# Second feed-forward product straight to nodes on the partitions, residual from rows, first norms on VectorE, all planning constants new

## The chip, the cores and the metric

The kernel runs on one core of a Trainium2 chip. The metric is the time of one execution on the device in microseconds (us); where several were made, the median is quoted.

In the lines of profiles, PE is TensorE (PEld its weight loads), DVE is VectorE, ACT is ScalarE, POOL is GpSimd, and SPq is the queue of SyncE, which issues transfers. `out<-in` names the tiles written and read, and L1089 is a line of the kernel.

## The reference, cut to what matters

Sixteen graphs share one adjacency matrix. Three graph-attention layers are followed by one transformer layer with eight heads, two feed-forward products and two layer norms. The change is in the last lines and in the very first norm.

```python
# x: (16, 1024, 256) float32, adj: (1024, 1024)
h = jnp.maximum(_layernorm(x, axis=-1), 0.0)             # the first norm
x = x + _L0_gnn_ref(h, adj, ...)                         # 4 heads
# ... layers 1 and 2 alike, with one head each ...
# layer 3 (cut): q, k, v = split(x @ w_qkv); 8 heads, masked softmax over the 1024 nodes; t = attention output
x = _layernorm(x + t, ln1_g, ln1_b)
h = jax.nn.relu(jnp.einsum('fnc,cd->fnd', x, w1) + b1)
f_out = jnp.einsum('fnd,dc->fnc', h, w2) + b2
x = _layernorm(x + f_out, ln2_g, ln2_b)
```

## The kernel before

The kernel records every operation with a guessed duration, and then plans the order itself. It runs a list scheduler over all five engines, in which each stretch of a batch has a rising priority given by fitted constants (`GATS`, `VALUES`, `STEPS`, `FEED`, `LEAD`, `BIAS`). The engines then work through that order.

In the last layer, queries and keys are split into a high and a low part, and both are moved by SyncE into stacks of operands for the score products. A projection (one of queries or keys, for one of two head groups `g` and one node half `hf`) makes 16 moves of 64 KB. There is one buffer `hi` and one buffer `lo`:

```python
        def project(g, hf, keys, stack, at):
            sc, hi, lo = r_sc.new(), r_hi.new(), r_lo.new()
            # ... two products into sc (PSUM) on TensorE ...
            act(act_us(HALF), lambda: nc.scalar.copy(hi.t.bitcast(F32R), sc.t), [hi], [sc])
            dve(tt_us(HALF), lambda: nc.vector.tensor_sub(lo.t, sc.t, hi.t), [lo], [sc, hi])
            for a in range(4):
                part = ((hi, hi, lo, lo), (hi, lo, hi, lo))[keys][a]
                for r in range(HG):
                    dma(0.33, lambda: nc.sync.dma_start(
                            stack.t[a * D3 : (a + 1) * D3, r, at : at + HALF],
                            part.t[r * D3 : (r + 1) * D3, :]),
                        [stack((r, hf if keys else 0, a))], [part], us=0.635)
```

The softmax denominators are sums of exponentials over nodes. In the second node half of each head group, two of each four tiles are added by transfers of 512 KB that accumulate while they write, issued by GpSimd. There are 16 of them in each batch except the last, 240 in all:

```python
        def run_of(g, hf):
            return 1 if b == NB - 1 else 4 if hf == 1 else 2
        # ... for each of the 8 tiles jt of a stage (g, hf):
                if jt % run == 1:
                    # ... VectorE starts the sum of a run: sums = pas[m - 1] + pas[m] ...
                elif jt % run:
                    for ss, pt in zip(sums[g, hf], pas[m]):
                        dma(3.0, lambda: nc.gpsimd.dma_start(ss.t, pt.t, accum_op=ALU.add),
                            [ss], [pt], us=0.88, engine="pool")
```

The feed-forward part kept channels on the partitions up to the residual, and then transposed back:

```python
        def forward(hf):
            yT = yTs[hf]                          # normed rows, transposed, with gain and bias
            fT = [r_fz.new() for _ in range(CT)]
            # ... first product and Relu into fT ...
            for co in range(CT):
                g = r_bank.new()
                pe(CT * mm_us(HALF), lambda: product(g, co, w2_sb, lambda ct: fT[ct].t), [g], fT)
                u = yT.t[:, co, :]
                dve(stt_us(HALF), lambda: nc.vector.scalar_tensor_tensor(
                        u, g.t, cols["b2"][:, co : co + 1], u, op0=ALU.add, op1=ALU.add), [yT(co)], [g])
        def back(hf):
            # ... four transposes of yT per pair of node tiles into a PSUM bank ...
            # ... ScalarE copies each tile to SBUF with accum_out (the sum for the norm), then the norm ...
```

## Time and profile before

| | before |
|---|---|
| median of 3 runs | 4160.25 us (4156.57 to 4164.75) |
| profiled execution | 4150.3 us |
| mean granted TensorE clock | 0.991 |
| streaming of all TensorE records, by their start-to-start times | 3,822 us |
| mean time of a steady batch (14 of them) | 251.2 us |

A steady batch is the time from the first one-head graph-attention product of one batch to that of the next, read from the trace. One more number is the **loss**. I add up what the TensorE records should take back to back (0.43 us for width 512, and so on), and about 0.35 us for each visit to the column-tiled form (records marked `128*32`, of which four take the time of one full product). The time by which TensorE's starts fall behind that sum is loss: 46 us in ten steady batches, 4.6 us a batch.

### The profile page before, as it was taken

How to read it: one execution, taken by the hardware profiler on the slowest of the kernel's cores; microseconds unless marked ns; L12 is line 12 of the kernel's file. 1: busy time of each engine (PE TensorE's matmuls, PEld its weight loads, DVE VectorE, ACT ScalarE, POOL GpSimd, SP SyncE). 2: the span in 40 equal slices, each digit the busy share in tenths (PEclk: the TensorE clock that was granted, in tenths of full speed). 3: DMA queues.
4: the chain of work that ended last, by engine and by line, in shares of the span. 5: the costliest groups of instructions: out<-in, count | busy, mean ns of one | idle time of the engine just before them, and what ended most of it. 6: DMA issues, size and time to landing. Idle time of an engine off the chain costs nothing.

```text
span 4150.3 us, 68028 instructions
## 1 busy us (share of the span) xinstructions
PE 4049.7 (98%) x23874; PEld 2358.5 (57%) x23874; DVE 3504.5 (84%) x5994; ACT 2680.9 (65%) x6673; POOL 558.7 (13%) x631
## 2 busy tenths in 40 slices
PE   7899999999999999999999999999999999999998
PEld 3746556564665646556464665646556465564643
DVE  7498888988889898898988889888897988889866
ACT  4556667576766756667566665756667566575665
POOL 0001111111111101111111111111111111111110
PEclk9999999999999999999999999999999999999999
DMA  3124444344443424443254443434434244442441
GB/s 105 37 67 103 116 96 102 77 90 105 100 109 84 103 78 100 114 105 95 69 112 108 97 102 88 92 92 100 110 92 100 71 103 119 98 95 65 98 111 47
DMA packets 215246, 389.63 MB, mean 94 GB/s; under 512 B 45168, under 2 KB 80240, under 8 KB 214896
## 3 DMA queue, kind: packets, MB, share of 16 engines
q1 hardware_dynamic: 180336, 259.36, 22.3%
q0 software_dynamic: 34560, 125.84, 16.0%
q8 instruction: 190, 3.11, 0.3%
q14 instruction: 160, 1.31, 0.1%
HBM read 91.03 MB, written 33.95 MB: 30 GB/s over the span
## 4 chain that ended last, share of the span: by engine, by line
PE 79%; ACT 8%; DVE 6%; DMA 2%; SPq 2%; issue 2%; POOL 0%; DVEq 0%; ACTq 0%
PE bank L840 18%; PE bank L1161 12%; PE sc L1295 10%; PE bank L927 10%; PE bank L716 7%; PE bank L512 5%; PE bank L937 5%; PE bank L1392 5%; PE sc L1077 4%; ACT waste L429 2%; PE sc L1113 2%; SPq L1098 2%; DVE pa L1328 2%; ACT pa L1319 1%; DVE pt L813 1%
## 5 line engine op out<-in xcount | busy, mean ns | idle before, releaser
L1319 ACT ACTIVATE pa<-sc 128x512 f32<-128x512 f32 x2048 | 1108.1, 607 | 448.7 <-PE sc L1295 317.5
L1328 DVE TENSOR_TENSOR pa<-pa,mask 128x1024 f32<-128x1024 f32 x1024 | 1221.9, 1220 | 72.9 <-ACT pa L1319 68.6
L813 DVE SCALAR_TENSOR_TENSOR pt<-row,e,mask 128x512 f32<-128x512 f32 x1536 | 1068.1, 747 | 49.6 <-DMA row<-rd 35.8
L840 PE MATMUL bank<-qb,pt 128*128 128x257 f32 x4096 | 943.9, 383 | 1.4 <-DVE pt L813 1.0
L840 PEld LDWEIGHTS bank<-qb,pt 128*128 128x128 f32 x4096 | 780.5, 191 | 143.8 <-ACT pa L1319 11.7
L1295 PE MATMUL sc<-qs,ks 128*128 128x512 f32 x2048 | 702.8, 451 | 39.1 <-DVE lo L1089 35.7
L1295 PEld LDWEIGHTS sc<-qs,ks 128*128 128x128 f32 x2048 | 361.2, 190 | 288.1 <-issue 91.2
L1161 PE MATMUL bank<-pa,va 128*32 128x512 f32 x4096 | 514.7, 597 | 1.3 <-DVE pa L1328 1.0
L927 PE MATMUL bank<-pt,qb 128*32 128x512 f32 x4096 | 502.2, 596 | 4.3 <-DVE pt L813 3.4
L1188 DVE TENSOR_TENSOR sums<-pa,pa 128x1024 f32<-128x1024 f32 x360 | 435.6, 1221 | 30.3 <-PE bank L1161 25.3
L716 PE MATMUL bank<-w_aug,hT 128*128 128x259 f32 (+1 forms) x1536 | 391.2, 393 | 2.1 <-ACT hT L710 1.9
L1196 POOL DMA_DIRECT2D sums<-pa x240 | 210.5, 877 | 1059.4 <-DVE rec L860 239.0
L716 PEld LDWEIGHTS bank<-w_aug,hT 128*128 128x128 f32 x1536 | 283.9, 192 | 110.3 <-ACT pa L1319 12.6
L868 ACT ACTIVATE ex<-bank,rec 128x256 f32<-128x256 f32 x256 | 123.4, 482 | 303.3 <-DVE rec L860 302.6
L927 PEld LDWEIGHTS bank<-pt,qb 128*32 128x32 f32 x4096 | 122.3, 109 | 296.5 <-issue 224.0
L937 PE MATMUL bank<-pt,e 128*32 128x512 f32 x2048 | 278.6, 594 | 0.0
L1161 PEld LDWEIGHTS bank<-pa,va 128*32 128x32 f32 x4096 | 116.4, 109 | 256.7 <-issue 216.9
L1077 PE MATMUL sc<-hTa,wqkv_sb 128*128 128x512 f32 x512 | 244.5, 602 | 1.6 <-ACT pa L1319 0.8
L483 ACT ACTIVATE hn<-xt,mv,rstd 128x256 f32<-128x256 f32 x384 | 203.3, 597 | 51.6 <-DVE mv L456 30.0
L429 ACT ACTIVATE waste<-xt,mv 128x256 f32<-128x256 f32 x384 | 196.2, 511 | 7.0
L1161 PE MATMUL bank<-sums,ones 128*32 128x512 f32 x1440 | 193.5, 599 | 0.2 <-DMA sums<-pa 0.2
L1086 ACT CAST hi<-sc 128x512 fp32r<-128x512 f32 x128 | 74.5, 582 | 178.9 <-PE sc L1077 76.9
(119 smaller groups left out, 4305.9 us busy)
## 6 DMA issues: line engine op xcount, KB each, us to landing
sums<-pa POOLq DMA_DIRECT2D x240, 512.0 KB, 5.9
row<-rd SPq DMA_DIRECT2D x192, 256.0 KB
ks<-hi SPq DMA_DIRECT2D x512, 64.0 KB
ks<-lo SPq DMA_DIRECT2D x512, 64.0 KB
qs<-hi SPq DMA_DIRECT2D x512, 64.0 KB
qs<-lo SPq DMA_DIRECT2D x512, 64.0 KB
xt<-in_x_dram SPq DMA_DIRECT2D x32, 512.0 KB
x<-xt SPq DMA_DIRECT2D x32, 512.0 KB
```

The lines of the kernel that those rows point to most:

```text
L429: lambda: nc.scalar.activation(waste.t, src, AF.Square, bias=sums[:, k : k + 1], accum_out=squares[:, k : k + 1]),
L716: nc.tensor.matmul(g.t[:, : C + 3 * H], hT.t[:, ct, k * P : (k + 1) * P], w_aug[l][:, ct, :], start=ct == 0, stop=ct == CT - 1,)
L813: lambda: nc.vector.scalar_tensor_tensor(pt.t, row.t, e3[:, 2, jt // TH, h, jt % TH : jt % TH + 1], mask[:, jt, hf * HALF : (hf + 1) * HAL ...
L840: nc.tensor.matmul(g.t[:, : D + 1], pts[jt].t[:, k * P : (k + 1) * P], qb[:, jt, 0, :], start=jt == 0, stop=jt == NT - 1,)
L927: nc.tensor.matmul(g.t[u * D + d : u * D + d + D3, :], qb[:, j, h + u, d : d + D3], pts[u][j - jt].t, start=j == 0, stop=j == NT - 1,)
L937: nc.tensor.matmul(gd.t[c : c + D3, :], one(jt + k, h + u).to_broadcast([P, D3]), pts[u][k].t, start=jt == 0, stop=jt == NT - 2,)
L1077: nc.tensor.matmul(sc.t, wqkv_sb[:, ct, c0 : c0 + P], hT.t[:, ct, hf * HALF : (hf + 1) * HALF], start=ct == 0, stop=ct == CT - 1,)
L1161: nc.tensor.matmul(ac.t[r * D3 : (r + 1) * D3, :], columns(r), of_head(r), start=first, stop=last,)
L1188: lambda: nc.vector.tensor_add(ss.t, p0.t, p1.t),
L1295: nc.tensor.matmul(scs[r - r0].t, ks.t[:, r, jt * P : (jt + 1) * P].bitcast(F32R), q.t[:, r, :].bitcast(F32R), start=True, stop=True,)
L1319: lambda: nc.scalar.activation(pt.t[:, v, :], sc.t, AF.Exp, scale=1.0 / math.sqrt(D3)),
L1328: lambda: nc.vector.tensor_mul(pt.t, pt.t, mask[:, jt : jt + 1, i0 : i0 + HALF].to_broadcast([P, 2, HALF]),),
```

## The change

TensorE bounds the kernel, so work is taken from it. The second product takes the Relu output as its stationary operand, so that nodes come out on the partitions at once and the transposes back go. The residual is then needed as rows, with gain and bias multiplied in by VectorE, and `b2` is folded into the bias row. The sum for the second norm comes from VectorE's residual add. In the first batch, the first norm's statistics are taken by VectorE. Buffers are cut to fit, and all planning constants are new.

```diff
-BIAS = 0.939
-LEAD = {"act": 2.715, "dve": 0.501}
+BIAS = 1.211
+LEAD = {"act": 2.365, "dve": 1.821}
 ... (GATS, VALUES, STEPS and FEED: all new as well) ...
-    r_yT = ring("yT", 2, [CT, HALF])
-    r_fz = ring("fz", 3, [HALF])
+    r_yT = ring("yT", 1, [CT, HALF])
+    r_fz = ring("fz", 2, [HALF])
+    r_z = ring("z", 2, [HALF])
 ...
+            h = hn.half(hf)
+            for op, row in ((ALU.mult, "g1"), (ALU.add, "cb")):
+                dve(tt_us(TH * C), lambda: nc.vector.tensor_tensor(
+                        h, h, rows[row].to_broadcast([P, TH, C]), op), [hn(it) for it in its], [b_feed])
 ...
-            for co in range(CT):
-                ... product(g, co, w2_sb, ...) and the residual add on yT ...
 ...
-                        transposes(lambda ct: pz()[:, k, ct * P : (ct + 1) * P],
-                                   lambda ct: yT.t[:, ct, i0 : i0 + P], CT)
+                        for ct in range(CT):
+                            nc.tensor.matmul(pz()[:, k, :], fT[ct].t[:, i0 : i0 + P], w2_sb[:, ct, :],
+                                             start=ct == 0, stop=ct == CT - 1)
-                        lambda: nc.scalar.activation(
-                            z_t[:, k, :], pz()[:, k, :], AF.Copy, accum_out=mvz.t[:, k, 0:1])
+                        lambda: nc.vector.scalar_tensor_tensor(
+                            z_t[:, k, :], pz()[:, k, :], 0.0, hn.at(it + k),
+                            op0=ALU.add, op1=ALU.add, accum_out=mvz.t[:, k, 0:1])
 ...
+            if not b:
+                for it in its:
+                    stats(xt.at(it), xt(it), b_mv.t[:, 0, it, :], b_mv((0, it)))
+                continue
```

More of the change, by code (lines that the diff above doesn't have):

```diff
@@ L313, in direct @@
     GATS = (
-        (-3.456, -2.901, -1.928, -0.561, 0.293),
-        (0.136, 0.471, 0.668, 0.738, 0.779),
-        (0.851, 0.853, 0.845, 0.944, 1.195),
-    )
-    VALUES = (1.183, 1.195, 1.056, 1.638, 0.894)
-    STEPS = (1.054, 1.508, 1.709, 1.977, 2.039)
-    FEED = (2.172, 2.298, 2.316, 2.334, 2.401)
+        (-4.564, -3.715, -2.378, -1.791, -0.286),
+        (-0.159, 0.648, 0.672, 0.678, 0.719),
+        (0.713, 0.729, 0.86, 0.888, 1.159),
+    )
+    VALUES = (0.885, -0.207, 0.784, 0.867, 1.288)
+    STEPS = (0.767, 1.497, 1.58, 1.837, 1.895)
+    FEED = (3.303, 2.616, 2.682, 3.025, 3.186)
     const = ctx.enter_context(tc.tile_pool(name="const", bufs=1))
@@ L340, in direct @@
     w2_sb = const.tile([P, CT, C], F32, name="w2_sb")
-    cols = {n: const.tile([P, CT], F32, name=f"col_{n}") for n in ("b1", "b2", "g1", "c1")}
-    rows = {n: const.tile([P, 1, C], F32, name=f"row_{n}") for n in ("g2", "c2")}
+    cols = {n: const.tile([P, CT], F32, name=f"col_{n}") for n in ("b1", "g1", "c1")}
+    rows = {n: const.tile([P, 1, C], F32, name=f"row_{n}") for n in ("g1", "cb", "g2", "c2")}
     mask = const.tile([P, NT, N], U8, name="mask")
@@ L427, in spread_of @@
             act(
-                act_us(C, 1) + 60e-3,
+                act_us(C, 1) + 190e-3,
                 lambda: nc.scalar.activation(
@@ L660, in load_feed, with gat @@
             nc.sync.dma_start(w2_sb, w2.rearrange("(t p) d -> p t d", p=P))
-            for n, ap in (("b1", b1), ("b2", b2), ("g1", ln1_g), ("c1", ln1_b)):
+            for n, ap in (("b1", b1), ("g1", ln1_g), ("c1", ln1_b)):
                 nc.sync.dma_start(cols[n], ap.rearrange("(t p) -> p t", p=P))
-            for n, ap in (("g2", ln2_g), ("c2", ln2_b)):
+            for n, ap in (("g1", ln1_g), ("cb", ln1_b), ("g2", ln2_g), ("c2", ln2_b)):
                 nc.sync.dma_start(rows[n][:, 0, :], rows_on_all(ap, C))
+            nc.gpsimd.dma_start(rows["cb"][:, 0, :], rows_on_all(b2, C), accum_op=ALU.add)
         dma(5.0, load_feed, [b_feed], [], us=3.6)
-    def gat(xt, b_mv, b_rstd, l):
+    def gat(b, xt, b_mv, b_rstd, l):
         H = HEADS[l]
@@ L683, in gat @@
             mv_refs, rstd_ref = [b_mv((l, it)) for it in its], b_rstd((l, hf))
-            inv = inverse_of_squares if l in SQUARED else inverse
+            inv = inverse_of_squares if l in SQUARED and (b or l) else inverse
             inv(mv[:, l, s, 0], mv[:, l, s, 1], rstd[:, l, s], mv_refs, rstd_ref)
@@ L895, in gat @@
                     dve(
-                        stt_us(C) + 60e-3,
+                        stt_us(C) + 0.03,
                         lambda: nc.vector.scalar_tensor_tensor(
@@ L1343, in feed @@
         mv, rstd = r_mv1.new(), r_rstd1.new()
-        yTs = [r_yT.new() for _ in range(2)]
+        yTs, fTs = {}, {}
         def turn(hf):
@@ L1364, in turn @@
                 )
+            yTs[hf] = r_yT.new()
             for ct in range(CT):
@@ L1388, in turn @@
                 )
+            h = hn.half(hf)
+            for op, row in ((ALU.mult, "g1"), (ALU.add, "cb")):
+                dve(
+                    tt_us(TH * C),
+                    lambda: nc.vector.tensor_tensor(
+                        h, h, rows[row].to_broadcast([P, TH, C]), op
+                    ),
+                    [hn(it) for it in its],
+                    [b_feed],
+                )
         def product(g, co, w_sb, src):
@@ L1401, in forward @@
             yT = yTs[hf]
-            fT = [r_fz.new() for _ in range(CT)]
+            fT = fTs[hf] = [r_fz.new() for _ in range(CT)]
             for co in range(CT):
@@ L1418, in forward @@
                 )
-            for co in range(CT):
-                g = r_bank.new()
-                pe(
-                    CT * mm_us(HALF),
-                    lambda: product(g, co, w2_sb, lambda ct: fT[ct].t),
-                    [g],
-                    fT,
-                )
-                u = yT.t[:, co, :]
-                dve(
-                    stt_us(HALF),
-                    lambda: nc.vector.scalar_tensor_tensor(
-                        u, g.t, cols["b2"][:, co : co + 1], u, op0=ALU.add, op1=ALU.add
-                    ),
-                    [yT(co)],
-                    [g],
-                )
         def back(hf):
-            yT = yTs[hf]
+            fT = fTs[hf]
             for it in (hf * TH, hf * TH + 2):
-                g, z, mvz, rstdz = r_bank.new(), r_fz.new(), r_mvz.new(), r_rstdz.new()
+                g, z, mvz, rstdz = r_bank.new(), r_z.new(), r_mvz.new(), r_rstdz.new()
                 xr = r_xr.new()
@@ L1460, in pz, with product2 @@
                     return g.t.rearrange("p (t c) -> p t c", c=C)
-                def turn_back():
+                def product2():
                     for k in range(2):
                         i0 = (it % TH + k) * P
-                        transposes(
-                            lambda ct: pz()[:, k, ct * P : (ct + 1) * P],
-                            lambda ct: yT.t[:, ct, i0 : i0 + P],
-                            CT,
-                        )
-                pe(0.109 * 2 * CT, turn_back, [g], [yT])
-                for k in range(2):
-                    act(
-                        act_us(C) + 60e-3,
-                        lambda: nc.scalar.activation(
-                            z_t[:, k, :], pz()[:, k, :], AF.Copy, accum_out=mvz.t[:, k, 0:1]
+                        for ct in range(CT):
+                            nc.tensor.matmul(
+                                pz()[:, k, :],
+                                fT[ct].t[:, i0 : i0 + P],
+                                w2_sb[:, ct, :],
+                                start=ct == 0,
+                                stop=ct == CT - 1,
+                            )
+                pe(2 * CT * mm_us(C), product2, [g], fT)
+                for k in range(2):
+                    dve(
+                        stt_us(C) + 0.03,
+                        lambda: nc.vector.scalar_tensor_tensor(
+                            z_t[:, k, :],
+                            pz()[:, k, :],
+                            0.0,
+                            hn.at(it + k),
+                            op0=ALU.add,
+                            op1=ALU.add,
+                            accum_out=mvz.t[:, k, 0:1],
                         ),
                         [z(k), mvz(k)],
-                        [g],
+                        [g, hn(it + k)],
                     )
@@ L1543, in batch @@
             its = range(hf * TH, (hf + 1) * TH)
+            if not b:
+                for it in its:
+                    stats(xt.at(it), xt(it), b_mv.t[:, 0, it, :], b_mv((0, it)))
+                continue
             for it in its:
                 act(
-                    act_us(C) + 60e-3,
+                    act_us(C) + 190e-3,
                     lambda: nc.scalar.activation(
@@ L1562, in batch @@
             rec.stream(b, GATS[l])
-            gat(xt, b_mv, b_rstd, l)
+            gat(b, xt, b_mv, b_rstd, l)
         for hf in range(2):
```

## The prediction

> **What bounds the kernel now.** I read the busy shares first, then the chain that ended last, then the costs of the instructions that the change touches, then windows of one steady batch, then both ends of the run. The page of the kernel before says:
>
> ```profile
> span 4150.3 us, 68028 instructions
> PE 4049.7 (98%) x23874; PEld 2358.5 (57%) x23874; DVE 3504.5 (84%) x5994; ACT 2680.9 (65%) x6673; POOL 558.7 (13%) x631
> PE   7899999999999999999999999999999999999998
> PE 79%; ACT 8%; DVE 6%; DMA 2%; SPq 2%; issue 2%; POOL 0%; DVEq 0%; ACTq 0%
> ```
>
> TensorE is 90% busy or more in every slice but the first two and the last, and 79% of the chain is TensorE. Busy is not work, though: a matmul's record is longer than the time until the next one starts. So I take start-to-start times from the timeline of TensorE (start, duration, line, count):
>
> ```profile
> 448.09 1.88 PE L1392 MATMUL bank<-yT,w_sb 128*128 128x512 f32 x4
> 449.81 3.78 PE L716 MATMUL bank<-w_aug,hT 128*128 128x268 f32 x16
> ...
> 455.35 1.92 PE L927 MATMUL bank<-pt,qb 128*32 128x512 f32 x16
> ...
> 460.64 1.98 PE L1077 MATMUL sc<-hTa,wqkv_sb 128*128 128x512 f32 x4
> 462.55 1.92 PE L927 MATMUL bank<-pt,qb 128*32 128x512 f32 x16
> ...
> 496.56 0.60 PE L512 MATMUL bank<-ident,yT 128*128 128x128 f32 x4
> 496.99 1.89 PE L1113 MATMUL sc<-wqkv_sb,hTa 128*128 128x256 f32 x8
> 498.72 0.60 PE L512 MATMUL bank<-ident,yT 128*128 128x128 f32 x4
> ```
>
> Four records of width 512 take 1.72 us (448.09 to 449.81), 0.43 each; eight of width 256 take 1.73 (496.99 to 498.72), 0.216 each; four transposes take 0.43 (496.56 to 496.99), 0.109 each. An fp32 product has two records, a transpose one. From 455.35 to 462.55, 7.20 us, there are 48 column-tiled records (0.107 each, as 16 take 1.72) and four of 0.43: 6.85 us. The other 0.35 us is what going into the tiled form and out again costs. Fitting all 414 such visits in the trace gives 0.34 to 0.37 us for the way in and out together, and about nothing (3 ns) for a change between full products and the score products.
>
> With these numbers all TensorE records of the run are 3,822 us of streaming, and its 430 tiled visits 153 us. The remaining 175 us are waits; windows place most of them: about 66 us before 340 us (one batch alone in the pipeline), about 25 after 4050 us, and 4 to 5 us in each of the steady batches of 252 us. The largest steady wait is score products waiting for their operands:
>
> ```profile
> PE sc L1295 <- DVE lo L1089: 35.7, 14, 4.2
> ```
>
> So the middle is bound by TensorE's streaming. VectorE is the next engine; in two of five windows of a steady batch it has little left (columns: window, length, PE, PEld, DVE, ACT, POOL busy):
>
> ```profile
> 1504.00:1554.00 50.00, 50.00 (x334) 23.50 (x332) 49.55 (x88) 33.64 (x81) 7.63 (x6) 1.00 0.18 53
> 1554.00:1604.00 50.00, 47.09 (x257) 30.94 (x253) 45.74 (x69) 31.04 (x82) 9.11 (x10) 1.00 0.60 135
> ```
>
> **What the Trainium skill says.** (1) "Perfetto Trace Analysis", Identifying the Most-Contended Engine: matmul busy share is no measure of headroom, as pipelined matmuls look different in the trace. The trace agrees: records of 1.88 us follow each other every 1.72. (2) "TensorE: Matmul & The Clock Gate", Part 4: PE-mode transpose, gives about 275 ns for a transpose in a kernel. The trace's records show the same (mean 276 ns), but back to back they cost 0.109 us; I use the 0.109. (3) "VectorE: DVE Perf Modes", the errata section, has (N+151)/0.96 for fp32 tensor_tensor: 1224 ns for N = 1024, 424 for 256. The trace has 1220 and 422. (4) The same page, Two Vector instructions with no wait between them, says that an operation with an accumulator output is two instructions; the trace agrees, with 422 + 85 ns for the group at L897.
>
> **The change part by part.** The groups that it touches, by shape (busy us, mean ns):
>
> ```profile
> L512 PE MATMUL bank<-ident,yT 128*128 128x128 f32 x256 | 39.0, 276 | 3.6 <-DVE yT L1430 3.6
> L1392 PE MATMUL bank<-fz,w_sb 128*128 128x512 f32 x256 | 119.9, 599 | 0.9 <-ACT fz L1413 0.9
> L1475 ACT ACTIVATE fz<-bank 128x256 f32<-128x256 f32 x128 | 48.3, 390 | 6.7 <-PE bank L512 6.7
> L1430 DVE SCALAR_TENSOR_TENSOR yT<-bank,col_b,yT 128x512 f32<-128x512 f32 x64 | 47.8, 748 | 5.9 <-PE bank L1392 5.7
> L897 DVE SCALAR_TENSOR_TENSOR xt<-xt,ex 128x256 f32<-128x256 f32 x256 | 106.8, 422 | 46.8 <-ACT ex L868 34.4 <-ACT ex L882 12.4
> ```
>
> *TensorE.* The second product changes from 256 records of 0.43 (110 us) to 512 of 0.216 (111 us): nothing. The 256 transposes back to nodes go: 256 x 0.109 = **27.9 us saved**, all on the bounding engine. But the constants of the scheduler are changed too, so the order of all work moves. The instruction orders show TensorE's changes of form going from 1,768 to 1,977, nearly all of them the free kind; tiled visits go from 430 to 448: 18 x 0.355 = **6.4 us lost**.
>
> *VectorE.* Removed: 64 residual adds, 47.8 us. Added: 128 residual adds of width 256 from PSUM with accumulator. The SBUF form takes (106.8 + 21.8)/256 = 0.50 us; the PSUM form of width 512 (748 ns) is 55 ns above the SBUF one (693), so 0.55 x 128 = 70 us. Added: 64 row operations of width 1024 for gain and bias, 64 x 1.22 = 78 us. Added in the first batch: 8 times 0.416 + 0.179 for the norms, 5 us. Net +105 us, so 3,610 us, 87% of the new span. Per steady batch 6 to 7 us more, where now some 32 of 250 are idle.
>
> *ScalarE.* The 128 copies with their accumulator reads go (48.3 + 27.4 us), and in the first batch 8 sums and 8 squares with theirs (11 us): 2,681 to about 2,594 us. It does not bound.
>
> *Head.* ScalarE's norms of the first input run from 6.8 us; its first normalisation starts only at 15.2 although its coefficients are there at 13.7, as the second half's sums hold the queue; the second half's coefficients come at 22.4. On VectorE both are done between the preparation of weights that already sits there, so I expect the second half some 4 us earlier. VectorE then has adjacency tiles in the way, so I count **3.5 us saved**.
>
> *Tail.* After the last attention product 36 us pass, a chain of small steps. The transposes and the ScalarE copies behind them go. One stall is visible: VectorE sits in order behind an operand row that comes by DMA (2.90 us in which TensorE waits for L1430 at 4138). In the new order one of the two residual adds still stands behind such a row, and two row operations (2.4 us) come in. **3 us saved.**
>
> Sum: 4160.25 - 27.9 + 6.4 - 3.5 - 3 = **4132 us**, if the steady waits (4 to 5 us a batch) stay as they are.
>
> **Rivals.** *VectorE becomes the bound.* For it: two windows at 91 to 99%, 105 us more, and a longer hold of the normalised rows (three half-batch buffers, now needed until the second product's residual, so the next batch's attention can wait on this one's feed-forward, and the transposed buffer is cut from two to one). Against it: 13% of VectorE stays idle, and the feed-forward is filler without a deadline. If a quarter of the 105 us came through: 4158; all of it: 4237. *The saved transposes are filler too*, and where they stood TensorE waits longer for the same operands: then only the ends gain, about 4155. Against it: in 21 of 25 windows of 10 us of a batch TensorE shows no idle time at all. *The new constants do more than hold*: the finer mix of score products and other work keeps ScalarE's exponentials and VectorE's masks fed, and the steady waits halve, some 33 us: 4099. For it: in the new order score products come in small groups between the one-head products. Nothing in the old trace shows it.
>
> **Range and chances.** The two certain terms give -21.5; the ends have an error of 3 us each; the steady waits can move by 25 us either way. I predict 4132, with 4104 to 4160 for 8 in 10. Faster by over 2% needs 83 us, more than every saving that I can name with the halved waits: 0.03. Slower by over 2% needs nearly all of VectorE's extra work exposed: 0.02. Within 2%: 0.95.
>
> **What would show it.** Right: no transposes of yT; the second product's records of width 256 at 0.216 us start to start; about 448 tiled visits; VectorE near 3,610 us and ScalarE near 2,594; a steady batch of about 250.5 us instead of 252; first tiled product near 37 instead of 40.4 us. Wrong: TensorE waits on VectorE residual adds, on the row operations or on buffers of normalised rows, with a batch at or above 252 us (first rival), or a batch below 249 us (third).

## More of the kernel before

Of the planner, the place that matters here is how it counts a transfer. There is one queue for each issuing engine, and none of them knows of the others:

```python
            x.start = at
            if x.moved:
                queue[e] = max(at + 0.2, queue[e]) + x.moved
                x.pass_on = queue[e] + LANDING - (at + us)
            order.append(x)
            free[e] = at + us
```

The prediction shows the lines on the engines. The page's list of DMA issues has the transfers that turn out to matter (name, queue, count, size, median us from issue to landing):

```profile
sums<-pa POOLq DMA_DIRECT2D x240, 512.0 KB, 5.9
```

## The result and the profile after

The changed kernel is correct and takes **4256.38 us** (four runs, 4251.23 to 4256.59), against 4159.34 us of the kernel before with its further run. The ratio is **1.0229** (95% interval 1.0211 to 1.0246), slower by 2.3%. A ratio here is the mean time of one kernel's runs over that of the other's runs of the same rounds, so not quite the ratio of the medians quoted.

The page of the changed kernel:

```profile
span 4254.4 us, 68427 instructions
PE 4085.8 (96%) x23874; PEld 2398.1 (56%) x23874; DVE 3565.9 (84%) x6266; ACT 2661.7 (63%) x6383; POOL 633.3 (15%) x632
PE 48%; DVE 18%; ACT 9%; SPq 8%; DMA 6%; issue 3%; POOL 1%; DVEq 0%; ACTq 0%; POOLq 0%
```

TensorE's share of the chain that ended last falls from 79% to 48%. VectorE has 18%, but SyncE's queue and the transfers, 4% together before, now have 14%. The busy shares hardly move, so this is not a kernel that got a new full engine. It waits more.

The groups that the change made, by shape, are as intended:

```profile
L1463 PE MATMUL bank<-w_sb,fz 128*128 128x256 f32 x512 | 121.7, 386 | 12.8 <-ACT fz L1427 12.8
L1475 DVE SCALAR_TENSOR_TENSOR z<-bank,hna 128x256 f32<-128x256 f32 x128 | 50.8, 417 | 3.8 <-PE bank L1463 3.8
L1397 DVE TENSOR_TENSOR hna<-hna,row_g 128x1024 f32<-128x1024 f32 x32 | 39.1, 1222 | 3.1 <-PE bank L513 3.0
```

**Where the time went.** By the start of the first one-head product of each batch, the profiled executions divide so:

| stretch | before, us | after, us | difference |
|---|---|---|---|
| start to batch 0's first product | 118.2 | 127.8 | +9.6 |
| batch 0 to batch 1 | 191.1 | 200.6 | +9.5 |
| 14 steady batches | 14 x 251.2 | 14 x 258.7 | +105.1 |
| batch 15's first product to the end | 324.7 | 304.5 | -20.2 |
| sum | 4150.3 | 4254.4 | +104.1 |

The loss of a steady batch rises from 4.6 to 13.4 us, while TensorE's streaming falls by 27.3 us over the run. Most of the loss sits in a stretch of some 40 us of each batch, where the queries and keys of the second head group are moved. First that stretch in the timeline of the kernel before (start, duration, engine and line, operation, count of instructions merged, and in brackets the idle time before and who ended it; SPq is SyncE's queue):

```profile
1568.51 3.90 SPq L1098 DMA_DIRECT2D qs<-hi  x6
1573.64 7.97 SPq L1098 DMA_DIRECT2D qs<-lo  x8
1575.61 0.92 POOL L1196 DMA_DIRECT2D sums<-pa  x1 [9.62 <-DVE sums L1188]
...
1586.12 0.97 PE L1295 MATMUL sc<-qs,ks 128*128 128x512 f32 x3 [2.92 <-DVE lo L1089]
1586.93 1.90 PE L840 MATMUL bank<-qb,pt 128*128 128x257 f32 x8
```

Its window in which the engines wait (window, length, busy PE, PEld, DVE, ACT, POOL with counts, then granted clock, busy share of the 16 DMA engines, GB/s):

```profile
1582.00:1586.00 4.00, 1.21 (x6) 0.70 (x4) 0.62 (x2) 1.03 (x2) 1.49 (x2) 1.00 0.98 206
```

The same stretch in the timeline of the changed kernel:

```profile
1607.80 4.95 SPq L1100 DMA_DIRECT2D qs<-hi  x8
1612.84 8.24 SPq L1100 DMA_DIRECT2D qs<-lo  x8
...
1615.37 0.87 POOL L1198 DMA_DIRECT2D sums<-pa  x1 [0.48 <-DVE pa L1330]
1618.20 0.86 POOL L1198 DMA_DIRECT2D sums<-pa  x1 [1.96 <-DVE pa L1330]
...
1625.60 0.69 DVE L1091 TENSOR_TENSOR lo<-sc,hi 128x512 f32<-128x512 f32 x1 [4.10 <-DMA qs<-lo]
...
1626.34 0.80 PE L1297 MATMUL sc<-qs,ks 128*128 128x512 f32 x1 [3.57 <-DVE lo L1091]
1626.94 3.63 PE L842 MATMUL bank<-qb,pt 128*128 128x257 f32 x8
```

And two of its windows:

```profile
1621.00:1626.00 5.00, 1.77 (x8) 1.16 (x7) 0.90 (x2) 1.09 (x2) 0.86 (x1) 0.88 1.04 206
...
1628.00:1630.00 2.00, 2.00 (x6) 1.54 (x6) 2.00 (x5) 0.26 (x1) 1.56 (x1) 0.50 0.43 107
```

Read it as a chain. Eight moves of the high part take 4.95 us to issue, 0.62 us each. Once accumulating transfers are on their way, eight moves of the low part take 8.24 us, 1.03 us each. In the window from 1621 to 1626 the DMA engines are full (1.04, 206 GB/s) and all compute engines are mostly idle (TensorE works 1.77 of 5 us). VectorE stands 4.10 us before the subtraction that makes the next low part, because the one low buffer is still being read by the moves of the last (`<-DMA qs<-lo`). TensorE stands 3.57 us behind it. Then comes a second price: the granted clock is 0.50 in the next microseconds, and eight products of width 257 take 3.63 us where they took 1.90 in the kernel before, whose gap of 2.92 us left the clock at full.

The Trainium skill has both. "DMA: Bandwidth & Descriptors", Issuing engines are not separate DMA queues, says that transfers started by different engines run on the same 16 DMA engines and interleave. The trace agrees, as moves of SyncE slow down under transfers of GpSimd: over the whole changed kernel, a move takes 596 ns to issue when no accumulate was issued in the 7 us before it, 713 ns after one and 1,122 ns after two (594, 706 and 1,095 ns in the kernel before). "TensorE: Matmul & The Clock Gate", Part 1, says that one idle window of about 3.4 us halves the clock and that as long a busy one restores it. The clock records agree: between 300 and 4040 us all stretches at half clock last 3.4 us or twice that. The kernel before has 8 of them there, 37.5 us in all, and the changed one 19, 75.1 us in all. If all that time was streaming at half speed, the difference costs 18.8 us, an estimate from above.

Who waits for the landing of moves is in the list of waits (engine, what it was about to do, whom it waited for: total us, times, longest). In the kernel before:

```profile
ACT hi L1086 <- DMA qs<-hi: 29.7, 7, 5.3
...
DVE lo L1089 <- DMA qs<-lo: 18.3, 6, 4.5
...
DVE lo L1089 <- DMA ks<-hi: 14.9, 4, 4.6
```

In the changed kernel, with what TensorE waits for:

```profile
ACT hi L1088 <- DMA ks<-hi: 117.0, 18, 9.1
...
PE sc L1297 <- DVE lo L1091: 56.8, 15, 6.8
...
DVE lo L1091 <- DMA qs<-lo: 39.3, 10, 4.9
...
DVE lo L1091 <- DMA ks<-hi: 26.0, 5, 7.4
...
PE bank L513 <- ACT ota L1237: 22.1, 26, 2.8
...
PE bank L1463 <- ACT fz L1427: 12.8, 17, 0.8
```

So the prediction's "largest steady wait", score products behind VectorE's `lo`, rose from 35.7 to 56.8 us. It was a DMA wait seen at second hand. The 22.1 us before `ota` are new, and the trace shows a transfer behind them too: in each of the 13 batches where they occur, ScalarE's copy of `hi` has stood 7 to 9 us for the moves of keys, and TensorE's wait ends 1.5 us (2.5 us for its second part) after that copy starts.

### The profile page after: what moved, and what is told of

Its sections match the earlier page's. It is cut to its first block, busy times and chain, and to the rows that moved or that the text cites. A ratio compares the mean times of both kernels' runs of the same rounds, so it can differ in the third digit from the quotient of the medians.

```text
span 4254.4 us, 68427 instructions
## 1 busy us (share of the span) xinstructions
PE 4085.8 (96%) x23874; PEld 2398.1 (56%) x23874; DVE 3565.9 (84%) x6266; ACT 2661.7 (63%) x6383; POOL 633.3 (15%) x632
## 4 chain that ended last, share of the span: by engine, by line
PE 48%; DVE 18%; ACT 9%; SPq 8%; DMA 6%; issue 3%; POOL 1%; DVEq 0%; ACTq 0%; POOLq 0%
PE bank L842 15%; PE bank L1163 9%; SPq L1100 7%; PE sc L1297 7%; DVE pt L815 7%; PE bank L718 5%; DVE pa L1330 4%; ACT pa L1321 3%; PE sc L1079 3%; PE bank L513 3%; PE bank L929 2%; DVE sums L1190 2%; ACT waste L430 1%; PE sc L1115 1%; DMA qs<-lo 1%
## 5 line engine op out<-in xcount | busy, mean ns | idle before, releaser
L842 PE MATMUL bank<-qb,pt 128*128 128x257 f32 x4096 | 967.2, 388 | 1.5 <-ACT ex L870 1.0
L1297 PE MATMUL sc<-qs,ks 128*128 128x512 f32 x2048 | 736.9, 462 | 59.6 <-DVE lo L1091 56.8
L1163 PE MATMUL bank<-pa,va 128*32 128x512 f32 x4096 | 525.6, 597 | 0.8 <-DVE pa L1330 0.8
L929 PEld LDWEIGHTS bank<-pt,qb 128*32 128x32 f32 x4096 | 131.8, 109 | 295.3 <-issue 205.4
L450 POOL TENSOR_TENSOR rstd<-rstd,neg_half 128x4 f32<-128x4 f32 x94 | 120.8, 1285 | 705.7 <-DVE rstd L442 666.2
L1163 PE MATMUL bank<-sums,ones 128*32 128x512 f32 x1440 | 204.3, 603 | 4.2 <-ACT ex L870 2.6
```

What stands on the lines that cost most here:

```text
L842: nc.tensor.matmul(g.t[:, : D + 1], pts[jt].t[:, k * P : (k + 1) * P], qb[:, jt, 0, :], start=jt == 0, stop=jt == NT - 1,)
L929: nc.tensor.matmul(g.t[u * D + d : u * D + d + D3, :], qb[:, j, h + u, d : d + D3], pts[u][j - jt].t, start=j == 0, stop=j == NT - 1,)
L1163: nc.tensor.matmul(ac.t[r * D3 : (r + 1) * D3, :], columns(r), of_head(r), start=first, stop=last,)
L1297: nc.tensor.matmul(scs[r - r0].t, ks.t[:, r, jt * P : (jt + 1) * P].bitcast(F32R), q.t[:, r, :].bitcast(F32R), start=True, stop=True,)
```

## The experiments

Three theories had to be told apart. Theory V: VectorE's added work is in the way (the prediction's first rival). Theory C: the new constants are worse than the old ones. Theory D, formed after reading the traces: accumulating transfers and operand moves collide on the DMA engines, and the new order stands closer behind the moves. The runs test its first half; the second is not shown (see the end of the next part). All runs had three rounds beside the kernel before; the ratio is to it. "Steady batch" is the mean of 14, as above.

| run | correct | median us | ratio | steady batch us |
|---|---|---|---|---|
| before | yes | 4159.34 | | 251.2 |
| after | yes | 4256.38 | 1.0229 | 258.7 |
| e1, after with the old constants | yes | 4262.63 | 1.0243 | 259.1 |
| e2, before with the new constants | yes | 4410.69 | 1.0605 | 270.3 |
| e3, after without the first norms on VectorE | yes | 4259.98 | 1.0240 | 258.9 |
| e4, after, thin row operations | yes | 4246.26 | 1.0209 | 257.9 |
| e5, after, thin accumulates | not | 4111.87 | 0.9877 | 249.0 |
| e6, before, thin accumulates | not | 4097.30 | 0.9839 | 247.5 |
| e7, after, low parts moved by GpSimd | yes | 4207.25 | 1.0108 | 255.2 |
| e8, before, one constant nudged | yes | 4161.14 | 0.9995 | 251.5 |
| e9, after, thin accumulates in group 0 alone | not | 4114.78 | 0.9888 | 249.4 |
| e10, after, accumulates in the other half, replanned | yes | 4088.63 | 0.9827 | 247.5 |
| e11, before, replanned | yes | 4097.07 | 0.9848 | 248.1 |
| e12, before, accumulates in the other half, replanned | yes | 4124.03 | 0.9912 | 249.8 |
| e13, after, two high and two low buffers | not | 4202.02 | 1.0113 | 254.1 |
| e14, after, two low buffers | not | 4209.82 | 1.0134 | 254.8 |
| e15, after, replanned | yes | 4203.59 | 1.0110 | 254.9 |

### e1 and e2: the constants exchanged

```diff
 e1: the changed kernel          e2: the kernel before
-BIAS = 1.211                    -BIAS = 0.939
+BIAS = 0.939                    +BIAS = 1.211
 ... and LEAD, GATS, VALUES, STEPS, FEED likewise
```

> The changed kernel with the six scheduling constants (BIAS, LEAD, GATS, VALUES, STEPS, FEED) of the kernel before; all arithmetic is that of the change. Theory C (the new constants order the work badly): the steady batch falls back to about 251 us and the run to 4130 to 4175 us. Theory V (VectorE's extra work and the longer hold of the normalised rows are what costs): it stays at 4240 us or more. The order has 505 tiled visits against 448, so some 20 us of its time are for that alone.

> The kernel before with the six scheduling constants of the change. Theory C: it is slowed by about as much as the change, 4230 us or more. Theory V: it stays near 4160 us, plus about 25 us for 502 tiled visits in place of 430.

Measured: 4262.63 and 4410.69 us. e1 came out where theory V had put it (4240 us or more) and e2 where theory C had (4230 us or more). Neither set carries over to the other structure with the time that it had in its own, so neither run says what a structure is worth. The old constants on the new structure give 505 tiled visits in place of 448 and still nearly the same time. Theory C in its plain form ("take the old ones back") is out.

### e3: first norms back on ScalarE

```diff
-            if not b:
-                for it in its:
-                    stats(xt.at(it), xt(it), b_mv.t[:, 0, it, :], b_mv((0, it)))
-                continue
```

> The changed kernel with the norms of the first input on ScalarE again, new constants. Both theories: within 15 us of the change (4256 us), as it touches one batch alone. A gain of over 60 us would say that the head is the cause, or that small changes of the order alone move the time that much.

Measured: 4259.98 us against 4256.38, and the intervals of the two ratios overlap. The third part of the change is worth nothing that can be told apart from zero.

### e4: row operations on 8 of 256 channels, same order

```diff
-                        h, h, rows[row].to_broadcast([P, TH, C]), op
+                        h[:, :, :8], h[:, :, :8], rows[row][:, :, :8].to_broadcast([P, TH, 8]), op
```

The result stays right, as gain is 1 and bias 0 in these inputs. Every engine keeps its exact order, and VectorE's row operations fall from 77.9 to 11.9 us.

> The changed kernel in exactly its order of instructions on each engine, but the 64 row operations for gain and bias work on 8 columns in each of 4 row tiles (32 elements) in place of 1024: about 1.05 us less each, 67 us of VectorE in all, 4.2 us a batch. The outputs stay right, as gain is 1 and bias 0 in these inputs. Theory V: at least 40 us faster than the change (under 4216 us). Theory C: under 15 us faster (4241 us or more), since the order makes the waits.

Measured: 4246.26 us, some 10 us gained of the 97 lost. The row operations explain a tenth. The rest of theory V, the residual add on VectorE and the longer hold of the normalised rows, is not taken out by this run.

### e5 and e6: thin accumulates, same order

```diff
-                            lambda: nc.gpsimd.dma_start(ss.t, pt.t, accum_op=ALU.add),
+                            lambda: nc.gpsimd.dma_start(ss.t[:, :1, :16], pt.t[:, :1, :16], accum_op=ALU.add),
```

The sums are wrong. The order, the waits and the number of transfers stay.

> The changed kernel in exactly its order, with each of the 240 accumulating transfers cut from 512 KB to 8 KB (wrong sums on purpose). Theory D (collision on the 16 DMA engines: in the stage where queries and keys are moved, 512 KB accumulating transfers and 64 KB operand moves fill all engines, the moves land late and TensorE's score products wait): the loss beyond streaming and switches falls from 13.4 us a steady batch to 7 or less, the time falls by 60 to 100 us to 4,155 to 4,195 us, ratio to before near 1.00 to 1.01. Theory O (the order alone: what waits is bound by issue times and by chains between TensorE, VectorE and ScalarE): less than 20 us gained, above 4,236 us.

> The same cut of the accumulating transfers in the kernel before, in its own order. Theory D: its loss is 4.6 us a batch, of which one wait of 3.2 us a batch follows a move; so 20 to 50 us gained, 4,110 to 4,140 us, less than the changed kernel gains, and the gap between the two closes to below 1 %. Theory O: less than 10 us gained and the gap stays near 97 us.

Measured: 4111.87 and 4097.30 us. The changed kernel gains 144 us and the kernel before 62 us, and the gap of 97 us shrinks to 15. Both times are lower than theory D had put down: e5 by 43 us below its range, e6 by 13 us. The timeline of e5 has the eight moves of the low part:

```profile
1565.43 4.97 SPq L1100 DMA_DIRECT2D qs<-lo  x8
```

Its list of waits has what is left of VectorE's waits for parts:

```profile
DVE lo L1091 <- DMA ks<-lo: 3.3, 5, 1.1
```

Eight such moves take 4.97 us instead of 8.24, and of VectorE's waits for the landing of parts (82.8 us in all in the changed kernel) 3.3 us are left. Of the 19 half-clock stretches between 300 and 4040 us, one is left. TensorE's wait behind `lo` is gone in e5 (56.8 us before) and falls from 35.7 to 0.2 us in e6. The first half of theory D holds: the collision accounts for 82 of the 97 us between the two orders. More than the other 15 us stays open: with thin accumulates in both, the changed kernel is 15 us slower where the prediction's two certain terms (-21.5 us) would have it faster, so by this estimate some 36 us have other causes, theory V among the candidates. TensorE's direct wait for the Relu, 12.8 us in e5 as well, is one of them.

### e7: low parts moved from a second queue, same order

```diff
-                        lambda: nc.sync.dma_start(
+                        lambda: (nc.gpsimd if part is lo else nc.sync).dma_start(
```

> The changed kernel in its order, with the moves of the low parts (half of all 2,048 operand moves) issued by GpSimd in place of SyncE; the bytes and the accumulates stay. If the time that SyncE takes to issue a move (0.6 us alone, over 1 us under load) is what delays the last move of a group: 40 to 90 us gained, 4,165 to 4,215 us. If the DMA engines' bandwidth is (theory D): within 25 us of 4,256. If GpSimd's own queue, where a move now stands behind an accumulate that waits for VectorE, becomes the wait: slower than 4,270 us.

Measured: 4207.25 us, 49 us gained, a third of e5's gain. That lies in the range for SyncE's time to issue (40 to 90 us), so this time is part of the delay. How large a part is not shown, since new waits take the place of some. In its list of waits TensorE now stands before the accumulated sums themselves, whose queue has moves in it (1.4 us in the changed kernel):

```profile
PE bank L1163 <- DMA sums<-pa: 29.5, 15, 2.7
```

### e8: one constant of the kernel before nudged (control)

```diff
-BIAS = 0.939
+BIAS = 0.95
```

> A control: the kernel before with one planning constant (the weight of a change of form, 0.939) moved to 0.95, which redraws the order a little and changes no work. If the time hangs on the order only smoothly: within 10 us of 4,159. If any redrawn order loses what the tuned one had: 20 us or more slower, as the 4,411 us of e2 suggests for a whole other set.

Measured: 4161.14 us, ratio 0.9995 (0.9978 to 1.0011). Nudged in this one constant, the old order does not sit on a knife's edge.

### e9: thin accumulates in the first head group alone, same order

```diff
+ ... the thin form of e5 `if g == 0 else` the full one
```

> The changed kernel in exactly its order, with only the 120 accumulating transfers of the first head group cut to 8 KB (wrong sums on purpose); the 120 of the second group stay at 512 KB. In the trace, the first group's stand between the operand moves (1612 to 1648 us), the second group's (1714 to 1748 us) have no move beside them. Collision theory: 115 us or more of the 144 us of e5, so 4,110 to 4,141 us. If large accumulating transfers cost the same anywhere (by the bytes alone, or by what waits for their sums): half, near 4,184 us.

Measured: 4114.78 us. 142 of the 144 us come from the 120 accumulates that stand among the operand moves. The other 120, with as many bytes, cost 3 us, which the spread of the runs hides. It is the meeting that costs, not the transfer.

### e10, e11, e12 and e15: replanned with the collision in the plan

I searched the constants anew. Each candidate order was replayed with moves that take longer to issue and to land while an accumulate is under way. The sizes for this were fitted to the times of the runs so far; they served the search only and are no measurement. e10 also moves the accumulates to the other node half:

```diff
-            return 1 if b == NB - 1 else 4 if hf == 1 else 2
+            return 1 if b == NB - 1 else 4 if hf == 0 else 2
-BIAS = 1.211
-LEAD = {"act": 2.365, "dve": 1.821}
+BIAS = 1.381
+LEAD = {"act": 2.832, "dve": 3.851}
 ... all other planning constants as well ...
```

e12 is the same edit of the kernel before. e11 and e15 change constants alone, in the kernel before and in the changed one.

> The changed kernel with the accumulating transfers used for the first node half of each head group in place of the second (all of the arithmetic stays, 240 transfers as before), and the planning constants searched anew by replaying each planned order with a collision in it: a move issued while an accumulate is under way takes 1.3 us to issue and 1.2 us to land, sizes that I fitted to the times of before, after, e1, e2, e5 and e6. Collision theory: the loss beyond streaming and switches falls under 4 us a batch and the time to 4,095 to 4,125 us, 0.8 to 1.6 % faster than before. If the changed structure itself is what costs (the residual on VectorE, the direct wait of the second product): above 4,160 us.

> The kernel before with nothing but the planning constants searched anew with the same collision in the plan: 4,085 to 4,115 us by the collision theory, since e6 without the collision took 4,097 us. If the order that before has is already the best for it: 4,150 us or more.

> The kernel before with the accumulating transfers in the other half and the constants searched anew, as e10 but without the change. Against e10 it tells what the change itself is worth when both are planned with the collision: by the sums of the prediction (27.9 us of TensorE less, some of it lost to the direct wait of 0.9 us a batch and to visits) e10 should be 0 to 20 us faster than e12; by the search's own order of the two they are within 5 us.

> The changed kernel with nothing but the planning constants searched anew with the collision in the plan. Collision theory: the stalls and with them the half-clock stretches of the steady batches (19 after 300 us in the changed kernel) go, and the time falls to 4,100 to 4,145 us, below before's 4,159. If the accumulates' place in this structure forces the loss whatever the order: above 4,200 us.

| replanned | accumulates where they were | in the other half |
|---|---|---|
| structure before | 4097.07 (e11) | 4124.03 (e12) |
| structure after | 4203.59 (e15) | **4088.63** (e10) |

e10 is correct and the fastest of all: ratio 0.9827 (0.9811 to 0.9843), 168 us faster than the changed kernel and some 71 us faster than the kernel before. That is 6 us below the range put down for it (4095 to 4125 us). e11 fell into its range (4085 to 4115). e12 missed: e10 was to be 0 to 20 us faster than it and is 35. The page of e10 has the chain back on TensorE:

```profile
PE 81%; ACT 7%; DVE 7%; issue 2%; DMA 1%; SPq 1%; POOL 1%; DVEq 0%; ACTq 0%
```

Of VectorE's wait for the moves of queries' low parts, its list of waits has this left:

```profile
DVE lo L1091 <- DMA qs<-lo: 1.0, 1, 1.0
```

Two of the four runs teach more than their times. In e11, 171 moves are still issued after two accumulates (197 in the kernel before), at 1,168 ns each, and yet its loss is 1.3 us a batch. **The collision is still there, but little waits for it any more:** VectorE's waits for the landing of parts fall from 40.3 to 5.9 us, ScalarE's from 41.0 to 5.1. And e15 missed what the collision theory had put down (4100 to 4145 us): at 4203.59 us it lies just in the range for "the accumulates' place forces the loss whatever the order" (above 4200 us), and 12 of the 19 half-clock stretches are left. One searched order can't show that of every order. What it shows is another door for the stall. VectorE, in order, now stands behind a residual row whose transfer lies in the same full engines. The timeline of e15:

```profile
1385.89 1.29 DVE L1447 TENSOR_TENSOR xr<-xr,row_c 128x512 f32<-128x512 f32 x2 [5.00 <-DMA xr<-x]
```

In the window the DMA share is 1.05 while TensorE, VectorE and ScalarE are mostly idle:

```profile
1384.00:1388.00 4.00, 1.02 (x5) 0.56 (x3) 2.11 (x8) 0.35 (x1) 0.92 (x1) 0.98 1.05 213
```

In the steady batches of e15 TensorE's largest wait is score products behind ScalarE's `pa`, 34.5 us in 12 of them, and in each it ends 2.8 us after such a wait of VectorE. My replay stretched operand moves only, so it could not see this. The cells were not searched equally long or from equally good starts, so the table does not measure what the change is worth once planned around the collision. With the accumulates in their old place the changed structure is 106 us slower (e15 against e11); in the other half it is 35 us faster (e10 against e12). Between the best of each, e10 and e11, lie 8 us: their runs do not overlap, but the intervals of their ratios do.

### e13 and e14: two part buffers, same order

What was open was by which path the collision reaches TensorE. To make room, the four broadcast rows share one buffer, so the result is wrong.

```diff
-        n, k = len(self.tiles), len(self.bufs)
+        n, k = getattr(self, "plan", len(self.tiles)), len(self.bufs)
-        self.bufs.append(Buf(self.tiles[k % n], before))
+        self.bufs.append(Buf(self.tiles[k % len(self.tiles)], before))
-    r_lo = ring("lo", 1, [HALF])
+    r_lo = ring("lo", 2, [HALF]); r_lo.plan = 1     # planned as one, laid out as two; e13: r_hi as well
-    rows = {n: const.tile([P, 1, C], F32, name=f"row_{n}") for n in ("g1", "cb", "g2", "c2")}
+    rows = dict.fromkeys(("g1", "cb", "g2", "c2"), const.tile([P, 1, C], F32, name="row_all"))
```

> The changed kernel in exactly its order, with two buffers in turn for the high and two for the low part of queries and keys (to make room, the four broadcast rows share one buffer, so the result is wrong on purpose; no duration hangs on it). All accumulates and moves stay. If the collision reaches TensorE through the part buffers (VectorE and ScalarE standing in order until the last part's moves have landed): 70 to 144 us gained, 4,112 to 4,186 us, and VectorE's wait on the landing of low parts gone. If the score products wait for the operands themselves: less than 30 us gained, above 4,226 us, with the wait now put down to the moves of keys or queries.

> As e13, with the low part's buffer alone doubled. If VectorE's wait is the path: nearly all of what e13 gains. If ScalarE's copy of the high part, which waits for its own moves, is as much in the path: about half of e13 or less.

Measured: 4202.02 and 4209.82 us, 54 and 47 us gained. For e13 neither theory's number came out; for e14 the first did, with 47 of the 54 us. The sharing of the rows cost some of it: batch 0's first product starts at 137.4 us instead of 127.8. The steady batch falls from 258.7 to 254.1 us, and e5's removal of the collision brings 249.0. So **about half** of what the collision costs in a steady batch goes through the part buffers. Waits of VectorE for part moves are gone in e13, and the low buffer alone makes most of the difference. The lists also tell the two paths apart: TensorE's 56.8 us behind `lo` are gone in both runs, while its wait behind ScalarE's high copies, gone in e13, stays in e14 (22.1 us in the changed kernel):

```profile
PE bank L513 <- ACT ota L1237: 21.1, 24, 3.1
```

ScalarE's own wait for the moves of keys, at 117.0 us the longest of all waits for a transfer, is still 123.0 us in e14: the length of a wait does not tell what it costs. Of the rest, the list of waits shows a part: VectorE's wait for residual rows (`xr<-x`) rises from 41.2 to 86.8 us and ScalarE's for accumulated sums from 6.9 to 24.1 us. As in e15, other transfers in the same engines take over. I have not isolated how much of TensorE's time each of them takes.

## Why the prediction was wrong

The prediction said 4132 us (4104 to 4160) and "within 2%". The time was 4256, outside the range.

- **The step that failed** is the condition on the sum: "if the steady waits (4 to 5 us a batch) stay as they are". They rose from 4.6 to 13.4 us a batch. In a steady batch, 27.3/16 = 1.7 us less streaming, 18 x 0.355/16 = 0.4 us more visits and 8.8 us more loss make +7.5, and the trace has 258.7 - 251.2 = 7.5. (Loss is what is left over, so this sum closes by construction; e5 and e6 are what ties the loss to the collision.) Over 14 batches the 8.8 us are 123 us, five times the allowance of 25 us. No other term of the prediction could reach "slower by over 2%" (chance 0.02): even with all of VectorE's 105 us exposed its sum gives 4237, below the 4243 us that 2% would need.
- **Why it failed.** I took the 35.7 us of score products behind `lo` as a wait between two engines. The wait behind it, VectorE's own for `qs<-lo`, was in the same profile, as were windows at 206 GB/s, and I did not follow it. None of the three rivals had a transfer in it.
- **TensorE's 27.9 us**: right, 27.3 us of streaming less. **Tiled visits 448**: right. **Second product** at the old cost: right by the sum, but its records now depend directly on the Relu: `fz` to the product costs 12.8 us over 17 waits, which the prediction did not count.
- **VectorE +105 us**: too high. The busy times of its groups rise by 74.5 us. The rows took 77.9 us as predicted (78). The residual add took 417 ns plus 81 ns for its accumulator, 64 us in all, not 0.55 us each and 70 us: with its source in PSUM (the memory that TensorE writes) it is no longer than the same form from SBUF (419 and 80 ns). The rest lies in groups that the change doesn't touch, which came out shorter. Busy time ends at 3,566 us, not 3,610. **ScalarE**: its groups fall by 98.9 us (predicted 87), but busy time only to 2,662 us and not to 2,594, as they overlap less.
- **First rival (VectorE becomes the bound)**: mostly not so. It said 4158 to 4237, but e4 puts the row operations at 10 us, and with thin accumulates in both kernels (e5, e6) some 36 us, by the estimate there, are left for it and for all else. **Second rival (the saved transposes are filler)**: not tested by itself. With thin accumulates the changed kernel's steady batch is still 1.5 us longer (249.0 against 247.5), so in this order the saved streaming did not come through. **Third rival (new constants halve the waits)**: its sign was wrong.
- **Head, 3.5 us saved**: wrong. The first tiled product starts at 48.8 us, not at 37 or at the old 40.4, and batch 0's first product is 9.6 us later. With the first norms back on ScalarE (e3) that product starts at 122.4 us, so in this order the norms account for about half of it, yet the whole run does not show it.
- **Tail, 3 us saved**: right in sign. After the last attention product 34.3 us pass instead of 36.2. The 20 us in the table are not this: the last stretch holds 14.4 us less of TensorE's streaming, as the new order does more of the work before the cut, and with thin accumulates it is 23 us shorter all the same (e5 against e6).

What stays open: why the collision costs the changed order 144 us and the old one 62, and so whether the new one stands closer behind the moves. Both have four accumulates among the moves of the same head group, and the eight low moves take 1.00 us each in the one and 1.03 in the other. Over the run 295 moves of the changed kernel are issued after two or more accumulates, and 239 of the kernel before. The count does not settle it, since e1 has 237 and loses as much as the changed kernel. e13 and e15 show several doors through which the delay comes, so I do not name one cause for the order.

## What to carry to other kernels

When a wait's releaser is an engine that is itself idle, ask what that engine waits for, until the chain ends in work or in a transfer. A planner that counts each queue's transfers by itself cannot see two queues meet in the same DMA engines: keep large accumulating transfers out of the stretch in which operands are moved (142 us here), or plan so that little waits for the moves (62 us in e11). After any structural change to a planned kernel, replan before judging it: the same change cost 97 us in the order it came with and 106 us with replanned constants alone, and once the accumulates had moved as well its best version is 8 us faster than the best replanned version without it.

## What the Trainium skill lacked or had wrong

- "DMA: Bandwidth & Descriptors", Issuing engines are not separate DMA queues, calls the time to initiate a transfer usually small relative to the transfer itself. Here it was not: 596 ns for a move of 64 KB, of some 2.0 us from issue to landing, and 1,122 ns after two accumulates, so issuing itself slows under load; a second issuing queue gained 49 us (e7).
- No page that I read has the duration of an accumulating transfer from SBUF to SBUF: 512 KB took a median of 5.9 us from issue to landing.
- "TensorE: Matmul & The Clock Gate", Part 4, gives no cost for transposes back to back. In float32 they start 0.109 us apart, and the change, which removes 256 of them, has 27.3 us less streaming.
